# A smaller-products step at two places of a two-layer cross attention, with a bias sum moved to other engines and one load moved ahead

## The chip, the cores and the metric

The kernel runs on one core of one Trainium2 chip. The time is device time in microseconds (us) of one execution of the whole program, everything in float32. Five engines work side by side, each through its own queue in order: TensorE (PE, matrix products; its weight loads are shown apart as PEld), VectorE (DVE), ScalarE (ACT), GpSimd (POOL) and SyncE (SP, which here only issues DMA transfers). They wait for each other through semaphores. Sixteen DMA engines move data between the chip's memory (HBM) and the core's on-chip memory (SBUF).

## The reference

Eight batches of 100 tokens with 1024 features (x) attend twice to eight contexts of 1444 rows with 512 features (ctx). In short:

```python
Q, K, V = x @ Wq + bq, ctx @ Wk + bk, ctx @ Wv + bv        # layer 0, 1024 hidden
x = x + softmax(Q @ K.T / 32, over keys) @ V @ Wo + bo
q, k, v = x @ Wq1 + bq1, ctx @ Wk1 + bk1, ctx @ Wv1 + bv1  # layer 1
w = softmax(q @ k.T / 32, over the TOKENS)                 # axis=1
x = layernorm(w @ v + x) * gamma + beta
```

## The kernel before

The kernel never forms K or V. Scores are x Wq Wkᵀ ctxᵀ, so it multiplies the weights first (1024 x 512, one product per layer), applies that product to the tokens ("queries", called g here) and then multiplies g by the transposed context. The weighted rows of the context are multiplied afterwards by Wv Wo (another product of weights) in layer 0 and by Wv in layer 1. The biases give small additional vectors: of the key bias, the sum over h of WqT's rows times bk (1024 wide) is wanted in layer 0 only much later, as a bias of each token's scores.

The stages, in order of time:

- `qk0`, 0 to 53 us: the product of Wq and Wkᵀ of layer 0, while its weights load
- `vo0`, 53 to 99 us: the product of Wv and Wo of layer 0
- queries of layer 0, 99 to 135 us
- `qk1`, 135 to 182 us: the product of Wq and Wkᵀ of layer 1
- scores, softmax and weighted rows of layer 0 for the eight batches, 182 to 306 us. Scores of a later batch alternate with weighted rows of an earlier one
- projection by the product of Wv and Wo, 306 to 353 us, then queries of layer 1 up to 398 us, with the first batch's layer-1 scores in between
- the batches of layer 1, and a tail with the last layer norm up to 572 us

**Products by seven.** Each large product (weights or queries) is cut into 2 x 2 blocks A11 to A22 and B11 to B22 and done with seven block products instead of eight. The sums of blocks that this wants are called S1 to S4 (left) and T1 to T4 (right). The products have names that also show in the profile: X (first A11·B11, later more is accumulated on it), Z, Y = S1·T1, W, and the last one, called q. `put` copies a finished block from the accumulators to SBUF on ACT, `add` adds one on DVE. Some of the seven products are themselves done by seven smaller ones (`inner_product`), whose parts the profile shows as, for instance, `qk_q_x`, `qk_q_z` and so on. `half_steps` (L170) is the place that issues nearly all matmuls of products, so its line stands for all of them. `inner_product` yields after each smaller product, and `weight_products` uses that to interleave them with matmuls of another product (V). In `vo0` and `qk1` ("deep" in the code), Y is already done by seven smaller products. In `qk0` it is one product. In the queries of layer 1 the last product, S4·B22 added to Y (profile name g_y), is one product.

**Sums of scaled rows.** `scaled_copies` (L634) makes ACT write row times a scalar into one buffer each. `transfer_added` (L629) makes POOL issue a DMA from SBUF to SBUF that adds one buffer to another, 512 KB each time. `scaled_sum` builds a tree of these two. In `qk0` the first four of the key bias' eight terms go this way, and the other four are added on DVE (function `second_half`).

**What sets the order.** PE, ACT and POOL run in the order in which the program is written. DVE's order is chosen by a scheduler except where `vector.in_order` is set. SP issues loads in program order (`loaded_in_order`, L944), each waiting until its room in SBUF is free and until the transfers under way fit in 1800 KB. Rooms are taken from pools by tag: the eight weight rooms of `qk0` are followed by those of `vo0` (loads at L383 and L384, named vo in the profile), and those by the context's blocks (cT, transposed, four of them per batch, 128 features x 1444 rows each). `load_features(1, (2,))` loads the second batch's four blocks in the order 0, 1, 2, 3, where block 2 lies in a buffer of another tag (`prob`, three of them, also used by the bias sums).

Of the kernel before, what the change touches and what calls it, by code (L numbers as in the profile page):

```python
# [42 lines left out]
GT = G * T  # L43
TILES = ((0, 128), (128, 128), (256, 112), (368, 112), (480, 96), (576, 96), (672, 128))
SETS = ((2, (0, 1), range(0, 256)), (4, (2, 3), range(256, 480)), (6, (4, 5), range(480, 800)))
LATER = {(1, 4): 4, (1, 6): 4, (1, 7): 4}
ROWS = [range(8, 11), range(0, 4), range(4, 8)]
REST = range(11, 12)
FIRST, SECOND = (0, 3, 5), (1, 4, 6)
# [9 lines left out]
def two_layer_cross_attention(ctx: ExitStack, tc: tile.TileContext, a: dict, out: bass.AP):  # L59
# [294 lines left out]
    def weight_products(name, left, right, l_width, r_width, scaled, between=None):  # L354
# [32 lines left out]

        accs = {}

        def accumulate(side):  # L390
            for v, of in scaled:
                if of != side:
                    continue
                width = (l_width, r_width)[side]
                first = 0 if side == 0 else l_width
                srcs = [(units[h][:, first : first + width], cols[v][:, h : h + 1]) for h in range(EC)]
                if width == E:
                    accs[v] = transferred_sum(f"{name}_{v}", srcs, name)
                    continue
                acc = work.tile([P, L], F32, tag="half", name=f"{name}_{v}", bufs=1)  # L400
                accs[v] = acc
                if early:
                    tiles = [acc] + [t[:, i * L : (i + 1) * L] for t in prob for i in range(2)]
                    scaled_sum(tiles + [weight_rows(f"{name}_{v}_7")[:, :L]], srcs)
                    continue
                for h, (src, by) in enumerate(srcs):
                    if h == 0:
                        vector.tensor_scalar(acc, src, by, None, ALU.mult)
                    else:
                        vector.scalar_tensor_tensor(acc, src, by, acc, ALU.mult, ALU.add)  # L410
# [86 lines left out]
        if name == "qk0":  # L497

            t2, t4 = (weight_rows(f"{name}_t{n}") for n in (2, 4))
            T2, T4 = ([t[:, i * rh : (i + 1) * rh] for i in range(H)] for t in (t2, t4))  # L500
            Z = pair("z")
            product(Z, A12, B21, True)
            combine(T2, B22, T1, ALU.subtract)
            combine(T4, B21, T2, ALU.subtract)
            combine(S1, A21, A22, ALU.add)
            add(0, 0, Z)
            accumulate(1)
            W = pair("w")
            product(W, A22, T4, True)
            accumulate(0)  # L510
            put(1, 0, W)
        elif not deep:
            combine(S1, A21, A22, ALU.add)
            Z = pair("z")
            product(Z, A12, B21, True)
            accumulate(0)
        t = wide_sums(f"{name}_t")
        if deep:

            T2, S2, T4 = B11, A11, B21  # L520
            first, rest = slice(0, H - 1), slice(H - 1, H)
            combine(S1[first], A21[first], A22[first], ALU.add)
            for some in (first, rest):
                if some is rest:
                    combine(S1[some], A21[some], A22[some], ALU.add)
                combine(B12[some], B22[some], B12[some], ALU.subtract)
                combine(T2[some], B22[some], T1[some], ALU.subtract)
            Z = pair("z")
            product(Z, A12, B21, True)
            next(side, None)  # L530
            combine(A21, A11, A21, ALU.subtract)
            combine(S2, S1, A11, ALU.subtract)
            V = half_steps(X, S2, T2, False, nb, rh)
            for n, _ in enumerate(inner_product(f"{name}_y", S1, T1, nb, rh, t[:, 768:1536], *parts(1, 1))):
                run(islice(V, 2 * nb // (2 if n == 1 else 4)))
                if n == 1:
                    add(0, 0, Z)
                elif n == 3:
                    combine(T4, B21, T2, ALU.subtract)
                if n > 2:  # L540
                    next(side, None)
            run(V)
            put(0, 1, X)
        else:
            Y = pair("y")
            product(Y, S1, T1, True)
            put(1, 1, Y)
            vector.in_order = name != "qk0"
            combine(B12, B22, B12, ALU.subtract)
            if name != "qk0":  # L550
                T2, T4 = B11, B21
                combine(T2, B22, T1, ALU.subtract)
                add(0, 0, Z)
            combine(S1, S1, A11, ALU.subtract)
            S2 = S1
            combine(A21, A11, A21, ALU.subtract)
            if name != "qk0":
                combine(T4, B21, T2, ALU.subtract)
            product(X, S2, T2, False)
            put(0, 1, X)  # L560
        vector.in_order = True
        if name == "qk0":
            accs[scaled[0][0]][1]()
        V = half_steps(X, A21, B12, False, nb, rh)
        _, more = parts(0, 1)

        def last():
            combine(A12, A12, S2, ALU.subtract)
            if deep:
                for j in range(2):  # L570
                    to = block(0, 1, j)
                    vector.tensor_tensor(to, to, block(1, 1, j), ALU.add)
            else:
                add(0, 1, Y)
            return inner_product(f"{name}_q", A12, B22, nb, rh, t[:, 768:1536], more, more)

        if name == "qk0":
            run(islice(V, 2 * nb))
# [21 lines left out]
    def transferred_sum(name, srcs, of):  # L600

        n = EC if of == "qk1" else EC // 2
        tiles = [row(f"{name}_{n}") for n in range(2)] + [weight_rows(f"{name}_2")[:, :E]]
        tiles += [t[:, :E] for t in prob]
        if of != "qk0":
            tiles += [weight_rows(f"{name}_{n}")[:, :E] for n in range(6, 8)]
        if of == "qk1":  # L610
            tiles = [tiles[i] for i in (0, 3, 1, 4, 2, 5, 6, 7)]
        scaled_sum(tiles[:n], srcs[:n])

        def second_half():
            t = tiles[n]
            if of != "qk0":
                scaled_sum(tiles[n:], srcs[n:])
            else:
                for i, (src, by) in enumerate(srcs[n:]):
                    if i == 0:  # L620
                        vector.tensor_scalar(t, src, by, None, ALU.mult)
                    else:
                        vector.scalar_tensor_tensor(t, src, by, t, ALU.mult, ALU.add)
            transfer_added(tiles[0], t)

        return tiles[0], second_half

    def transfer_added(to, t):
        nc.gpsimd.dma_start(out=to, in_=t, accum_op=ALU.add)  # L629
# [83 lines left out]
    def key_bias_rows(kb, part, bqbk):  # L713

        n = B * T // QD
        ps = bank("kb")[:, :n]
        for h in both_sides():
            nc.tensor.matmul(ps[h * HP : (h + 1) * HP], same[:, h * HP : (h + 1) * HP], part, start=True, stop=True)
        vector.tensor_scalar(part, ps, SCALE, bqbk, ALU.mult, ALU.add)
        spread = part.unsqueeze(2).to_broadcast([P, n, QD])  # L720
        vector.transpose(kb.rearrange("p (n i) -> p n i", i=QD), spread)

    def queries(layer, w, u, between=None):

# [42 lines left out]

        t = None

        def inner(n, lhs, rhs, put, add, right=None, at=0, left=None):  # L770
            spare = bank if layer else bank2
            return inner_product(f"g{layer}_{n}", lhs, rhs, nb, GT, t[:, at:], put, add, right, left, spare=spare)

        def four(t):

# [2 lines left out]
        def steps():  # L778
# [85 lines left out]
                vector.in_order = False  # L864
            else:
                run(V)
                add(1, 0, X)
                add(1, 1, X)
                vector.in_order = False
                yield  # L870
                product(Y, S4, B22, False)
                add(0, 1, Y)
            yield

        return dst, steps()
# [76 lines left out]
    def load_features(b, blocks=(2, 3), parts=2):  # L952

        bounds = [LAST * i // parts for i in range(parts)] + [S]

        for k in range(LC):
            name = f"cT_{b}_{k}"
            t = feature_block(name) if k in blocks else unit(name)[:, :S]
            for part in (slice(i, j) for i, j in zip(bounds, bounds[1:])):
# [585 lines left out]
                next(A, None)  # L1545
            yield

    cT = [list(load_features(0)), list(load_features(1, (2,)))]
    c0, more = list(load_rows(0)), load_features(2)
    cT.append([next(more)])  # L1550
    scores0 = scores_by_keys(batches[0], 0, cT[0], softmax0)
    run(islice(scores0, 3 * MC + 6))
    key_bias_rows(kb0, part0, bqbk0)
    run(scores0)
    cT[2] += more
    block_sums("u1", acc_u, sums[:, :LC, :], late=True)
# [40 lines left out]
    run(more)  # L1597
    vector.in_order = False
    part = key_bias_parts(kb1)
# [9 lines left out]
    tiles = [{"t0": t0, "n": n} for t0, n in TILES]  # L1609
    turned = turned_blocks(tiles)  # L1610
    scores1 = scores_by_keys(batches[0], 1, cT[0], softmax1, hold=True)
    run(islice(scores1, LC * MC))
    key_bias_rows(kb1, part, bqbk1)
    run(scores1)
    run(steps)
    run(scores_by_keys(batches[1], 1, cT[1], softmax1))

    finished = {
# [67 lines left out]
```

## Time and profile before

| | |
|---|---|
| runs | 573.16, 574.49, 570.84 us (median 573.16) |
| profiled execution | 574.2 us, its span 572.4 us |
| granted TensorE clock | 0.996 |
| PE busy | 561.5 us (98%) |
| DVE, ACT, POOL busy | 447.5, 146.0, 113.0 us |
| DMA moved | 141.24 MB, mean 247 GB/s |

The span runs from the first to the last recorded instruction; the execution's own time is 1.8 us longer. Busy time of an engine is the time in which at least one of its instructions ran. A row like `25.75 6.91 PE qk_y L170 x32` in the chain of waits reads: from 25.75 us on, for 6.91 us, the chain lies on 32 matmul records of PE that write the tile qk_y, issued at line 170. Each float32 matmul stands as two records. A group such as `vo<-vo,vo 128x512 f32<-128x512 f32` reads: output tile, then inputs, then shapes as partitions x elements; in brackets stands idle time before it and what ended it. In rows by window the figures are the stretch and its sum, then busy time of PE, PEld, DVE, ACT and POOL in us with the number of instructions, then the clock, the mean busy share of the 16 DMA engines, and GB/s.

### The profile page before, as it was taken

Reading aid. Unit: us, or ns where it says so; the run is one execution under the profiler, and the core shown is the slowest. Engines: PE = TensorE matmul, PEld = TensorE weight load, DVE = VectorE, ACT = ScalarE, POOL = GpSimd, SP = SyncE. Lnnn points to the kernel's source line nnn. Section 1 sums busy time; section 2 is a strip of 40 time slices with the busy share of each in tenths; the row PEclk is TensorE's granted clock in tenths of the full one; section 3 lists DMA queues with packets and bytes.
Section 4 is the critical chain, followed back from the end, with each engine's and each line's share of the span. In section 5 each row is a group of like instructions: output and inputs, shape, how many; then the busy total and the mean of one; then the engine's idle time right before and its main releaser. Section 6 shows DMA issues by size and latency. Waiting matters only on the chain.

```text
span 572.4 us, 17304 instructions
## 1 busy us (share of the span) xinstructions
PE 561.5 (98%) x7316; PEld 470.1 (82%) x7316; DVE 447.5 (78%) x1035; ACT 146.0 (26%) x383; POOL 113.0 (20%) x171
## 2 busy tenths in 40 slices
PE   9999999999999999999999999999999999999994
PEld 8888567668999999999998856678999869959672
DVE  1996979878989794976458687796688779879865
ACT  1331321356020112222011000122333035336632
POOL 3110110223100043242122000000421312403232
PEclk9999999999999999999999999999999999999998
DMA  8959989958839999999999603985799969985804
GB/s 278 315 110 326 315 197 285 320 87 198 212 58 321 351 314 318 316 338 308 309 319 347 209 1 134 281 297 189 232 301 331 334 226 330 300 279 169 216 8 92
DMA packets 73390, 141.24 MB, mean 247 GB/s; under 512 B 8160, under 2 KB 29920, under 8 KB 73312
## 3 DMA queue, kind: packets, MB, share of 16 engines
q1 hardware_dynamic: 66592, 121.40, 63.1%
q0 software_dynamic: 6288, 18.20, 16.4%
q8 instruction: 58, 0.95, 0.7%
q10 hardware_dynamic: 432, 0.52, 0.3%
q14 instruction: 20, 0.16, 0.1%
HBM read 123.49 MB, written 6.03 MB: 226 GB/s over the span
## 4 chain that ended last, share of the span: by engine, by line
PE 84%; DMA 10%; issue 1%; DVE 1%; POOL 1%; ACT 1%; SPq 1%; DVEq 0%; POOLq 0%
PE s L1087 17%; PE A L1015 16%; DMA cT<-in_ctxT 10%; PE qk_x L170 7%; PE g_x L170 6%; PE vo_x L170 4%; PE o_x L170 3%; PE g_y L170 3%; PE o_x L1338 3%; PE qk_z L170 2%; PE o_y L1338 2%; PE o_y L170 1%; PE qk_w L170 1%; PE qk_y L170 1%; PE vo_z L170 1%
## 5 line engine op out<-in xcount | busy, mean ns | idle before, releaser
L1015 PE MATMUL A<-w,c 128*64 128x100 f32 (+2 forms) x3072 | 216.9, 249 | 0.0
L1015 PEld LDWEIGHTS A<-w,c 128*64 128x64 f32 (+2 forms) x3072 | 190.8, 137 | 3.0 <-issue 1.8
L1087 PE MATMUL s<-g0T,cT 128*64 128x100 f32 (+1 forms) x1472 | 108.9, 249 | 2.2 <-DMA cT<-in_ctxT 1.5
L1087 PE MATMUL s<-g1T,cT 128*64 128x100 f32 (+1 forms) x1472 | 109.4, 249 | 0.0
L1087 PEld LDWEIGHTS s<-g0T,cT 128*64 128x64 f32 (+1 forms) x1472 | 95.1, 136 | 2.9 <-DMA cT<-in_ctxT 1.9
L1087 PEld LDWEIGHTS s<-g1T,cT 128*64 128x64 f32 (+1 forms) x1472 | 94.8, 136 | 1.1 <-issue 1.1
L1305 POOL TENSOR_TENSOR part<-w 128x500 f32<-128x500 f32 x16 | 25.3, 1582 | 237.8 <-DVE rtotal L102 75.8
L1283 ACT ACTIVATE w<-w,negmax 128x100 f32<-128x100 f32 x96 | 34.9, 365 | 45.0 <-DVE negmax L102 44.8
L1151 ACT ACTIVATE w<-w 128x400 f32<-128x400 f32 (+2 forms) x32 | 12.7, 446 | 116.4 <-DVE w L102 105.6
L102 DVE STREAM_TRANSPOSE z<-xT 32x256 f32<-32x256 f32 x88 | 38.3, 436 | 1.4
L170 PE MATMUL qk_x<-qk 128*128 128x256 f32 x160 | 38.0, 382 | 0.0
L170 PEld LDWEIGHTS qk_x<-qk 128*128 128x128 f32 x160 | 29.1, 192 | 3.5 <-ACT qk L444 0.2
L1068 DVE RECIPROCAL rrow<-A 128x100 f32<-128x100 f32 x8 | 6.1, 768 | 22.3 <-PE A L1059 22.3
L170 PE MATMUL vo_x<-vo 128*128 128x512 f32 x48 | 23.3, 594 | 0.0
L102 DVE TENSOR_REDUCE most<-s 128x100 f32<-128x400 f32 (+1 forms) x24 | 12.5, 524 | 12.1 <-PE s L1087 11.6
L102 DVE SCALAR_TENSOR_TENSOR w<-s,kb 128x400 f32<-128x400 f32 (+2 forms) x32 | 14.1, 464 | 8.2 <-PE s L1087 7.8
L102 DVE TENSOR_TENSOR w<-w,rtotal 128x400 f32<-128x400 f32 (+2 forms) x32 | 18.1, 566 | 1.1
L1283 ACT ACTIVATION_READ_ACCUMULATOR w<-w,negmax 128x1 f32 x96 | 18.0, 187 | 0.0
L740 ACT ACTIVATE g1T<-g_x,k 128x400 f32<-128x400 f32 x4 | 2.4, 593 | 60.3 <-PE g_x L170 60.2
L1308 POOL TENSOR_TENSOR part<-part 128x100 f32<-128x100 f32 x32 | 15.8, 493 | 2.5
L102 DVE TENSOR_TENSOR qk<-qk 128x256 f32<-128x256 f32 (+2 forms) x26 | 14.4, 579 | 0.0
L170 PE MATMUL qk_z<-qk 128*128 128x256 f32 x64 | 14.1, 379 | 0.0
(484 smaller groups left out, 1001.7 us busy)
## 6 DMA issues: line engine op xcount, KB each, us to landing
c<-in_ctx SPq DMA_DIRECT2D x176, 256.0 KB, 5.1
cT<-in_ctxT SPq DMA_DIRECT2D x96, 176.0 KB, 4.6
cT<-in_ctxT SPq DMA_DIRECT2D x32, 370.0 KB, 5.2
cT<-in_ctxT SPq DMA_DIRECT2D x32, 352.0 KB, 4.8
cT<-in_ctxT SPq DMA_DIRECT2D x32, 194.0 KB, 4.8
vo<-in_L_xattn_Wo SPq DMA_DIRECT2D x8, 512.0 KB, 8.7
qk<-in_L_xattn_WqT SPq DMA_DIRECT2D x8, 512.0 KB, 5.1
qk<-in_L_xattn_WqT SPq DMA_DIRECT2D x15, 256.0 KB, 5.0
```

What stands on the lines that cost most here:

```text
L102: ins = getattr(nc.vector, op)(*args, **kw)
L170: nc.tensor.matmul(banks[n // per][:, n % per * width : (n % per + 1) * width], lhs[i][:, n * P : (n + 1) * P], rhs[i], start=(fresh and i ...
L740: nc.scalar.activation(dst[g][:, c, :], banks[j][:, :GT], AF.Identity, bias=u[:, c : c + 1])
L1015: nc.tensor.matmul(ps[h * HP : (h + 1) * HP, k * T : (k + 1) * T], block[rows, m % CQ, k * P + h * HP : k * P + (h + 1) * HP], s["w"][rows ...
L1068: nc.vector.reciprocal(r, ps[:, GT : GT + T])
L1087: nc.tensor.matmul(to, cT[k][:, o : o + n], q[:, k, t0 : t0 + T], start=(k == 0 and m % GM == 0), stop=(k == LC - 1 or (k == LC - 2 and no ...
L1151: nc.scalar.activation(rows, rows, AF.Exp)
L1283: ins = nc.scalar.activation(rows[:, i, :], rows[:, i, :], AF.Exp, bias=negmax[:, i : i + 1], accum_out=total[:, i : i + 1])
L1305: add(part, w[:, 0:5, :], w[:, 5:10, :], ALU.add)
L1308: add(part[:, 0, :], part[:, 0, :], more, ALU.add)
L1338: nc.tensor.matmul(ps[:n, :], lhs[0][:, i, :], rhs[0][:, i, :], start=(fresh and i == 0), stop=(i == 1), skip_group_check=True,)
```

## The change

There are four parts.

1. In `qk0` the product Y is done by seven smaller products, interleaved with the next one (X += S2·T2), in the way the deep stages do it. S2 and the small sums get rooms of their own (three more `wide_sums` buffers in turn). The last product's sum `add(0, 1, Y)`, from the accumulators, becomes a sum of two SBUF blocks. The second bias, bq, is summed in two halves of four terms.
2. The key bias' second four terms go from DVE to ACT (four scaled copies into `prob1`, `prob2`, `prob0` and a row buffer) and POOL (four accumulating transfers, where there was one), issued piece by piece between the smaller products. In all of this bias' sum there are seven such transfers instead of four.
3. The second batch's third key block (index 2) is loaded first; the order on SP is 2, 0, 1, 3.
4. In the queries of layer 1 the last product is done by seven smaller ones. The key bias' rows are made four scores earlier, and the first batch's softmax runs between the smaller products and not inside the scores.

```diff
-LATER = {(1, 4): 4, (1, 6): 4, (1, 7): 4}
+LATER = {(1, 0): 0, (1, 4): 4, (1, 6): 4, (1, 7): 4}
...
-            Y = pair("y")
-            product(Y, S1, T1, True)
-            put(1, 1, Y)
-            vector.in_order = name != "qk0"
-            combine(B12, B22, B12, ALU.subtract)
...
-            combine(S1, S1, A11, ALU.subtract)
-            S2 = S1
-            combine(A21, A11, A21, ALU.subtract)
...
-            product(X, S2, T2, False)
+            vector.in_order = True
+            late = accs[scaled[0][0]][1]()
+            rooms = [wide_sums(f"{name}_s2_{i}") for i in range(2)]
+            S2 = [t2[:, i * lh : (i + 1) * lh] for t2 in rooms for i in range(2)]
+            combine(S2, S1, A11, ALU.subtract)
+            Y = inner_product(f"{name}_y", S1, T1, nb, rh, t[:, 768:1536], *parts(1, 1))
+            V = half_steps(X, S2, T2, False, nb, rh)
+            for n, _ in enumerate(Y):
+                run(islice(V, 2 * nb // (2 if n == 1 else 4)))
+                if n in (1, 2, 5):
+                    next(late)
+                if n == 3:
+                    combine(B12, B22, B12, ALU.subtract)
+                elif n == 4:
+                    accumulate(1, range(H, EC))
+                    combine(A21, A11, A21, ALU.subtract)
+            run(V)
             put(0, 1, X)
...
-        if name == "qk0":
-            accs[scaled[0][0]][1]()
...
+        def second_half_in_turn():
+            t, u, v, w = tiles[n], tiles[n + 1], tiles[n - 1], tiles[1]
+            scaled_copies((t, u), srcs[n : n + 2])
+            transfer_added(t, u)
+            yield
+            scaled_copies((v,), srcs[n + 2 : n + 3])
+            yield
+            scaled_copies((w,), srcs[n + 3 :])
+            for to, src in ((v, w), (t, v), (tiles[0], t)):
+                transfer_added(to, src)
+            yield
...
-                product(Y, S4, B22, False)
-                add(0, 1, Y)
+                _, more = parts(0, 1)
+                Q = inner("q", S4, B22, more, more, four(T2[0]), ahead=True)
+                yield
+                yield from Q
...
-    cT = [list(load_features(0)), list(load_features(1, (2,)))]
+    cT = [list(load_features(0))]
+    block, *more = load_features(1, (2,), order=(2, 0, 1, 3))
+    cT.append([*more[:2], block, *more[2:]])
...
-    run(islice(scores1, LC * MC))
-    key_bias_rows(kb1, part, bqbk1)
+    rows = key_bias_rows(kb1, part, bqbk1)
+    run(islice(scores1, LC * (MC - 1)))
+    next(rows)
+    run(islice(scores1, LC))
+    vector.in_order = True
+    next(steps)
+    run(rows)
+    next(steps)
     run(scores1)
+    first_softmax = batches[0]["softmax"]
+    for n in (1, 2, 2, 1):
+        next(steps)
+        run(islice(first_softmax, n))
+    next(steps)
+    vector.in_order = False
     run(steps)
+    run(first_softmax)
```

More of the change, by code (lines that the diff above doesn't have):

```diff
@@ L388, in weight_products, with accumulate @@
         accs = {}
-        def accumulate(side):
+        def accumulate(side, some=range(EC)):
             for v, of in scaled:
@@ L399, in accumulate @@
                     continue
-                acc = work.tile([P, L], F32, tag="half", name=f"{name}_{v}", bufs=1)
-                accs[v] = acc
+                if some[0] == 0:
+                    accs[v] = work.tile([P, L], F32, tag="half", name=f"{name}_{v}", bufs=1)
+                acc = accs[v]
                 if early:
@@ L405, in accumulate @@
                     continue
-                for h, (src, by) in enumerate(srcs):
+                for h in some:
+                    src, by = srcs[h]
                     if h == 0:
@@ L506, in weight_products @@
             add(0, 0, Z)
-            accumulate(1)
+            accumulate(1, range(H))
             W = pair("w")
@@ L511, in weight_products @@
             put(1, 0, W)
[L512 to L516, printed above, removed]
         t = wide_sums(f"{name}_t")
@@ L544, in weight_products @@
         else:
-            Y = pair("y")
-            product(Y, S1, T1, True)
-            put(1, 1, Y)
-            vector.in_order = name != "qk0"
-            combine(B12, B22, B12, ALU.subtract)
[L550 to L553, printed above, removed]
-            combine(S1, S1, A11, ALU.subtract)
-            S2 = S1
-            combine(A21, A11, A21, ALU.subtract)
-            if name != "qk0":
-                combine(T4, B21, T2, ALU.subtract)
-            product(X, S2, T2, False)
+            vector.in_order = True
[15 more added lines that the diff above has]
+            run(V)
             put(0, 1, X)
         vector.in_order = True
-        if name == "qk0":
-            accs[scaled[0][0]][1]()
         V = half_steps(X, A21, B12, False, nb, rh)
@@ L568, in last @@
             combine(A12, A12, S2, ALU.subtract)
[L569 to L573, printed above, removed]
-                add(0, 1, Y)
-            return inner_product(f"{name}_q", A12, B22, nb, rh, t[:, 768:1536], more, more)
+            for j in range(2):
+                to = block(0, 1, j)
+                vector.tensor_tensor(to, to, block(1, 1, j), ALU.add)
+            room = t if deep else wide_sums(f"{name}_q_t")
+            return inner_product(f"{name}_q", A12, B22, nb, rh, room[:, 768:1536], more, more)
         if name == "qk0":
@@ L614, in second_half @@
         def second_half():
[L615 to L626, printed above, removed]
+            scaled_sum(tiles[n:], srcs[n:])
+            transfer_added(tiles[0], tiles[n])
+        def second_half_in_turn():
[9 more added lines that the diff above has]
+            yield
+        return tiles[0], second_half_in_turn if of == "qk0" else second_half
     def transfer_added(to, t):
@@ L721, in key_bias_rows @@
         vector.transpose(kb.rearrange("p (n i) -> p n i", i=QD), spread)
+        yield
     def queries(layer, w, u, between=None):
@@ L768, in queries, with inner @@
         t = None
-        def inner(n, lhs, rhs, put, add, right=None, at=0, left=None):
-            spare = bank if layer else bank2
-            return inner_product(f"g{layer}_{n}", lhs, rhs, nb, GT, t[:, at:], put, add, right, left, spare=spare)
+        def inner(n, lhs, rhs, put, add, right=None, at=0, left=None, ahead=False):
+            spare = bank if layer and not ahead else bank2
+            return inner_product(f"g{layer}_{n}", lhs, rhs, nb, GT, t[:, at:], put, add, right, left, ahead, spare)
         def four(t):
@@ L866, in steps @@
                 run(V)
+                add(0, 1, Y)
                 add(1, 0, X)
@@ L870, in steps @@
                 yield
-                product(Y, S4, B22, False)
-                add(0, 1, Y)
+                _, more = parts(0, 1)
+                Q = inner("q", S4, B22, more, more, four(T2[0]), ahead=True)
+                yield
+                yield from Q
             yield
@@ L950, in loaded_in_order, with load_features @@
             tc.add_manual_dep(load, latest.name, landed, reason="room among the transfers under way")
-    def load_features(b, blocks=(2, 3), parts=2):
+    def load_features(b, blocks=(2, 3), parts=2, order=range(LC)):
         bounds = [LAST * i // parts for i in range(parts)] + [S]
-        for k in range(LC):
+        for k in order:
             name = f"cT_{b}_{k}"
@@ L1552, in two_layer_cross_attention @@
     run(islice(scores0, 3 * MC + 6))
-    key_bias_rows(kb0, part0, bqbk0)
+    run(key_bias_rows(kb0, part0, bqbk0))
     run(scores0)
@@ L1597, in two_layer_cross_attention @@
     run(more)
+    part = key_bias_parts(kb1)
+    next(steps)
     vector.in_order = False
-    part = key_bias_parts(kb1)
     wv1 = weights.tile([P, LC, E], F32, tag="w", name="wv1")
@@ L1611, in two_layer_cross_attention @@
     scores1 = scores_by_keys(batches[0], 1, cT[0], softmax1, hold=True)
-    run(islice(scores1, LC * MC))
-    key_bias_rows(kb1, part, bqbk1)
-    run(scores1)
+    rows = key_bias_rows(kb1, part, bqbk1)
[6 more added lines that the diff above has]
+    next(steps)
+    run(scores1)
+    first_softmax = batches[0]["softmax"]
+    for n in (1, 2, 2, 1):
+        next(steps)
+        run(islice(first_softmax, n))
+    next(steps)
+    vector.in_order = False
     run(steps)
+    run(first_softmax)
     run(scores_by_keys(batches[1], 1, cT[1], softmax1))
```

## The prediction

> **What bounds the kernel now.** I read the busy rows first, then TensorE's waits, then the chain that ended last, then the stages that the change touches, by window. Busy rows of the page:
>
> ```profile
> PE 561.5 (98%) x7316; PEld 470.1 (82%) x7316; DVE 447.5 (78%) x1035; ACT 146.0 (26%) x383; POOL 113.0 (20%) x171
> ```
>
> TensorE (PE) works 98% of the 572.4 us span. Its waits are all of this (engine, line, what it waited for: us in total, times, longest):
>
> ```profile
> PE s L1087 <- DMA cT<-in_ctxT: 1.5, 2, 0.9
> PE warm L114 <- DVE ones L111: 1.1, 1, 1.1
> PE s L1087 <- issue: 0.6, 1, 0.6
> PE ol L1498 <- ACT A1T L1030: 0.4, 1, 0.4
> ```
>
> 3.6 us in all. So the time falls only where matmuls go, and rises where a new wait appears. The stretches of the chain that the change replaces (start, us, what):
>
> ```profile
> 25.75 6.91 PE qk_y L170 x32
> ...
> 48.33 0.89 PE qk_q_y L170 x8
> ...
> 129.92 0.68 PE g_q_x L170 x4
> ...
> 392.50 5.57 PE g_y L170 x16
> ```
>
> Rows 1 and 4 are the two products that become seven smaller ones; rows 2 and 3 are one such smaller product of each width.
>
> **First stage, the product itself.** 32 records of 128x256 (6.91) become seven groups like row 2: 7 x 0.89 = 6.25 us. -0.66. Here a rule speaks against the change: the Trainium skill, "TensorE: Matmul & The Clock Gate", section "Back-to-back issue gap", gives about 81 ns per matmul at 128 columns and 131 at 512, so narrow ones cost nearly as much as wide ones. Interpolated (an estimate: 98 ns at 256), 56 narrow records against 32 would be 56 x 81 / (32 x 98) = 1.45 times, 6.91 to 10.0, +3.1. In the rows a record falls from 0.216 to 0.112 with half the columns, and the same exchange is seen in the second layer's first product. I take the rows.
>
> The seven are interleaved with the next product, so their sums must keep up. The key bias leaves VectorE (DVE): one of 0.66 and three of 1.20, 4.26 us between 31.3 and 36.9. What comes is some 14 sums, half of them 128x256 at 0.34 and half 128x128 at 0.20, 3.8 us, and two block sums of 0.34 for two sums of 0.60 gone. Replayed in order with these durations, the tightest sum is 2.8 us ahead of its matmul. ScalarE (ACT) takes four of 1.05; its copy of a smaller product stands behind the one that waits for a transfer landing at 33.3, and ends at about 34.7, 2.4 us ahead of need. No stall: 7 groups and the rest end 0.66 earlier, at about 52.1.
>
> **Its three further transfers.** The bias is now summed by accumulating DMAs of 512 KB that GpSimd (POOL) issues: seven, four before. This stage loads the next weights (vo) meanwhile. DMA shares, windows with start:end, then PE, PEld, DVE, ACT, POOL busy, clock, DMA share, GB/s:
>
> ```profile
> 36.00:42.00 6.00, 6.00 (x29) 5.06 (x28) 5.82 (x12) 2.99 (x4) 0.86 (x1) 1.00 0.63 119
> 42.00:48.00 6.00, 6.00 (x37) 5.46 (x36) 2.54 (x9) 1.42 (x2) 0.86 (x1) 1.00 1.01 248
> 48.00:54.00 6.00, 6.00 (x48) 5.43 (x48) 5.16 (x13) 1.15 (x1) 0.86 (x1) 1.00 1.00 381
> 54.00:62.00 8.00, 8.00 (x20) 3.54 (x19) 8.00 (x18) 2.66 (x4) 0.00 (x0) 1.00 1.01 289
> 62.00:66.00 4.00, 4.00 (x11) 1.78 (x10) 3.82 (x10) 2.68 (x3) 2.42 (x3) 1.00 1.05 397
> ```
>
> Up to 42 there is room, then the engines are full to past 66. From 34 to 42.4 two transfers took 66.0% of 8.4 us, 2.8 us of all engines each. The order of POOL's queue after: two old ones by 33.3, prob1+=prob2 at about 34, prob0+=bk1 at 36 (these fill the room), prob1+=prob0 once both landed, about 43, then bv0+=bv1 (42.56 before, now behind that wait), bk0+=prob1 after the landing before it, about 50, then bv2+=prob0 (53.03 before). So two extra, 5.5 us of DMA time, fall into full engines, beside vo_4 to vo_7, the last issued at 52.81. That one is waited for at once:
>
> ```profile
> 62.46 0.69 DVE L102 TENSOR_TENSOR vo<-vo,vo 128x512 f32<-128x512 f32 x1 [0.18 <-DMA vo<-in_L_xattn_Wo]
> ```
>
> It lands at 62.4. DVE needs 2.9 us more for the sum S2, so PE could have it at 65.4; PE wants it at 67.46 (66.8 with the 0.66 gained). PE then waits D = L - 63.9, L the landing. The skill's "DMA: Bandwidth & Descriptors", section "Issuing engines are not separate DMA queues", says that DMAs of all issuers interleave on the same 16 engines; the trace agrees (shares of both queues sum to 1.0), so the extra transfers do take from the loads. How much: from 42.4 to 62.4 the loads used 72.9% and the transfers 27.7%, 14.6 and 5.5 us. If both extra ones go ahead wholly, L = 67.9, D = 4.0; if bv2+=prob0 is pushed behind vo_7 in turn (2.6 us of it were served before 62.4), L = 65.3, D = 1.4; if the transfers starve while loads are queued, as from 50 to 57 where only loads moved, L stays near 62 and D = 0. I take the middle of the upper two, D = 2.3: prob1+=prob0 surely goes ahead (the window 46 to 48 had 88% for transfers while loads were queued), bk0+=prob1 in part. Bounds 0 and 4.0. Below nothing is excluded: the loads gain nothing.
>
> **Second batch's third key block first.** SyncE (SP) now sits 26.9 us at the block it loads first, while this stretch passes:
>
> ```profile
> 165.00:170.00 5.00, 5.00 (x36) 4.69 (x35) 5.00 (x15) 0.74 (x2) 0.00 (x0) 1.00 0.00 0
> ```
>
> No DMA at all. The block loaded first has a room free at about 142.2, so its 739 KB (2.1 us at the 345 GB/s of this stage's full slices) move out of the later stream. But PE waits for no DMA until 285.2; its two waits there (1.5 us) follow back through transfers to a room that PE itself frees at 230.4. Between is a stretch that is 0.96 full (190 to 300). Bounds: 0, and -1.5 if the stream runs ahead. I take 0, since the chain starts at a room and not at a transfer before it. The block competes with the second layer's key-bias load (issued 143.3, read at 156.1 by DVE): up to 2 us later, into 1.8 us of DVE idle at 158.2. Nothing.
>
> **Second layer, last product.** 5.57 becomes 7 x 0.68 = 4.76: -0.81. Sums added on DVE: four of 0.34 and four of 0.49, 3.3 us, after the key bias' row sums that end at 388.9 and with the softmax of the first batch moved behind, between the products. Replayed, the last three operands are ready 0.4 to 0.9 us ahead of PE. That margin is thin: the same form in this layer's z group took 5.14 where it waited for DVE, so the bound is -0.4. The key-bias matmul wants its input 1.7 us after it is ready; the softmax ends at about 403.5, before the weighted rows want it at 405.2. I take -0.81.
>
> **Sum.** -0.66 + 2.3 + 0 - 0.81 = +0.8. The profiled execution took 574.2 (572.4 and 1.8 around it), so 575.0; on the median of the three runs, 573.16, it is 574.0. A difference within 1% is what a measurement of this kernel can't tell from none.
>
> **Rivals.**
>
> A. As summed, some of the two transfers ahead of vo_7: D 1.0 to 4.0, 572.7 to 575.7. Chance 0.5.
>
> B. The transfers are hidden: D near 0. 573.16 - 1.47 = 571.7, and to 570.2 if the early block also takes away the waits at 285 and 294. For it: transfers got nothing from 50 to 57, and both landed late rather than the loads (10.0 us for bv2+=prob0). Against it: 46 to 48. Chance 0.32.
>
> C. Slower: ACT's in-order queue. Its copy prob1<-vo (60.41) must now wait until bk0+=prob1 has been read from prob1. Behind it stand four bias copies of 1.09 and then the copy of vo_y_x, at 67.66. If that transfer lands at time K, the copy comes at K + 4.4, and the products that read it move. It decides from K = 63.3, and beyond it each us costs PE one. Issued at 50 and taking 10 as bv2+=prob0 did, K = 60; served last, after 11 us of transfers and 14.6 of loads from 42.4, K = 68, and where packets of both go slower than apart (the shares run to 1.05), 71: D = 7.7, net +6.2, 579.4. Chance 0.15.
>
> D. The seven products do not pay: in the first stage a group waits for ACT's copy behind the transfer (slack 2.4), in layer two for DVE. Both gains gone with D = 2.3: 575.5. Chance 0.03, and inside the range.
>
> **Range.** 570.5 to 577.8: B's no-wait end at the bottom, and at the top A with D = 4 and 2 us more for the partly decided C. Left out are C's upper end and the best of B. Slower by over 1% (above 578.9) needs C fully: 0.10. Faster by over 1% (below 567.4) needs more than all gains together: 0.02.
>
> **What would show it.** The y groups with the interleaved product should stand from 25.75 to about 38.9 without a wait; no g_y row of 5.57 but seven of 0.68 near 392. DVE's wait for vo_7 should move from 62.46 to 64.9 to 67.9, followed by a new PE wait at vo_x of 1 to 4 us. If that wait is missing, B holds. If PE waits at the vo_y products for ACT, C holds. DMA should show a block of 739 KB soon after 143 and the wait of 26.9 us on SP should stay, at another block. Wrong would be: waits inside the seven products, DMA waits in the first layer's batches that grow because rooms come free in another order, or a clock below 0.996.

## The result, and the profile after

The changed kernel takes 577.63 us (median of 7 runs, 574.78 to 578.11) against 573.16 us before (7 runs, 570.84 to 575.31). The ratio is 1.0068, with a 95% interval of 1.0048 to 1.0089. By this ratio, which all the runs go into, it is slower by about 3.9 us (2.8 to 5.1); the two medians alone are 4.5 us apart. That is inside the range that was forecast and on the side of the forecast, but far more than the +0.8 us of its sum. The profiled execution has a span of 574.7 us, 2.3 us longer than before. That execution took 576.56 us, 1.1 us less than the median of its kernel; the profiled one of before took 1.0 us more than the median of its own.

First the busy row of the page, then TensorE's waits in the changed kernel (engine, line, what it waited for: us in total, times, longest):

```profile
PE 561.1 (98%) x7352; PEld 472.0 (82%) x7352; DVE 454.3 (79%) x1067; ACT 151.0 (26%) x389; POOL 115.8 (20%) x174
```

```profile
PE vo_z L170 <- DMA vo<-in_L_xattn_Wo: 1.9, 1, 1.9
PE vo_x L170 <- DVE vo L102: 1.3, 1, 1.3
PE warm L114 <- DVE ones L111: 1.1, 1, 1.1
PE g_x L170 <- ACT prob L633: 0.6, 1, 0.6
PE s L1091 <- DMA cT<-in_ctxT: 0.5, 1, 0.5
```

The first two rows are new: 3.2 us in the product of Wv and Wo, at two places. The waits for DMA in the first layer's batches are down from 1.5 to 0.5 us. The chain of waits shows the new stretch (start, us, what):

```profile
26.14 0.89 PE qk_y_x L170 x8
27.03 0.87 PE qk_x L170 x4
27.90 0.89 PE qk_y_z L170 x8
...
51.64 13.21 DMA vo<-in_L_xattn_Wo
64.85 0.14 issue
64.98 1.97 PE vo_z L170 x4
66.95 0.03 issue
66.98 0.69 DVE vo L102
67.67 0.34 DVE vo_s L102
68.01 2.89 DVE vo L102 x7
70.90 0.14 issue
71.03 1.10 PE vo_x L170 x2
```

The smaller products run without a wait. Then a load of Wo, issued at 51.64, needs 13.2 us to land, and after it the sums on DVE are late too. DVE itself, in order of time (start, us, engine, line, operation, tiles; in brackets the idle time before and what ended it):

```profile
56.98 0.76 DVE L102 TENSOR_TENSOR vo_s<-vo,vo 128x256 f32<-128x256 f32 x2
63.63 0.42 DVE L102 TENSOR_TENSOR vo_s<-vo,vo 128x256 f32<-128x256 f32 x1 [5.89 <-DMA vo<-in_L_xattn_WvT]
63.98 1.89 DVE L102 TENSOR_TENSOR vo<-vo,vo 128x512 f32<-128x512 f32 x3
65.78 1.89 DVE L102 TENSOR_TENSOR vo<-vo,vo_s 128x512 f32<-128x512 f32 x3
67.59 0.42 DVE L102 TENSOR_TENSOR vo_s<-vo,vo 128x256 f32<-128x256 f32 x1
67.92 0.68 DVE L102 TENSOR_TENSOR vo<-vo,vo 128x512 f32<-128x512 f32 x1
```

The third sum of this kind, which wants the WvT half of vo_6 (issued at 51.26), makes DVE stand still for 5.89 us. Before, the three sums ran without a wait:

```profile
57.25 1.09 DVE L102 TENSOR_TENSOR vo_s<-vo,vo 128x256 f32<-128x256 f32 x3
```

Everything behind the wait in DVE's order is late, down to the operand S2 that PE wants. By window (stretch, sum, busy us of PE, PEld, DVE, ACT, POOL with counts, clock, DMA share, GB/s), the same stretches as in the prediction:

```profile
36.00:42.00 6.00, 6.00 (x36) 5.32 (x35) 5.15 (x11) 2.60 (x4) 0.86 (x1) 1.00 1.04 196
42.00:48.00 6.00, 6.00 (x37) 5.49 (x36) 4.39 (x15) 2.30 (x2) 1.71 (x2) 1.00 0.94 280
48.00:54.00 6.00, 6.00 (x47) 5.28 (x46) 5.42 (x14) 1.15 (x1) 1.71 (x2) 1.00 1.05 256
54.00:62.00 8.00, 8.00 (x20) 3.41 (x19) 3.74 (x9) 2.69 (x4) 0.00 (x0) 1.00 1.06 298
62.00:66.00 4.00, 2.10 (x6) 0.76 (x5) 2.37 (x5) 1.74 (x2) 1.45 (x2) 1.00 1.03 368
```

The DMA engines were as full before from 42 on; what changed is whom they serve. In the list of queues, cut to 42.4 to 62.4 us (queue: packets, MB, share of 16 engines), before and then after:

```profile
q1 hardware_dynamic: 1962, 5.09, 72.9%
q0 software_dynamic: 297, 1.05, 27.7%
```

```profile
q1 hardware_dynamic: 1349, 3.65, 52.3%
q0 software_dynamic: 541, 2.01, 50.4%
```

The first queue holds the loads, the second POOL's transfers. The transfers' part rises from 5.5 to 10.1 us of all engines, and 1.44 MB of loads no longer arrive in this time.

Where the profile's 2.3 us went, by the start of the first matmul at each mark, after minus before: -0.3 at the start of the vo stage, +3.7 at the first vo_w_x, +4.4 at the second g_x product, +4.7 at the first weighted row, +2.4 at the projection of layer 0, +1.8 at the first weighted row of layer 1, +2.3 at the end. So from Z on the first stage gains 0.7 (Z itself came 0.4 later), the vo stage loses 3.9, the queries and the second product of weights 1.0, the batches of layer 0 give 2.3 back, and the last product of layer 1's queries 0.6.

### The profile page after: what moved, and what is told of

Read it like the earlier page. It is cut to its first block, busy times and chain, and to the rows that moved or that the text cites. A ratio compares the mean times of both kernels' runs of the same rounds, so it can differ in the third digit from the quotient of the medians.

```text
span 574.7 us, 17432 instructions
## 1 busy us (share of the span) xinstructions
PE 561.1 (98%) x7352; PEld 472.0 (82%) x7352; DVE 454.3 (79%) x1067; ACT 151.0 (26%) x389; POOL 115.8 (20%) x174
## 4 chain that ended last, share of the span: by engine, by line
PE 83%; DMA 10%; DVE 2%; issue 1%; ACT 1%; POOL 1%; SPq 0%; DVEq 0%; POOLq 0%; ACTq 0%
PE s L1091 19%; PE A L1019 18%; PE qk_x L170 7%; DMA cT<-in_ctxT 7%; PE g_x L170 5%; PE o_x L170 3%; PE o_x L1342 3%; PE vo_x L170 2%; PE qk_z L170 2%; DMA vo<-in_L_xattn_Wo 2%; PE o_y L1342 2%; PE g_y L170 2%; PE o_y L170 1%; PE qk_w L170 1%; DMA qk<-in_L_xattn_WkT 1%
## 5 line engine op out<-in xcount | busy, mean ns | idle before, releaser
L102 DVE TENSOR_TENSOR qk<-qk 128x256 f32<-128x256 f32 (+2 forms) x29 | 16.0, 585 | 0.0
L628 POOL DMA_DIRECT2D qk_L_xattn_bk<-qk_L_xattn_bk x6 | 5.2, 923 | 44.5 <-ACT qk_L_xattn_bk L633 17.6
```

The source lines that it names most:

```text
L102: ins = getattr(nc.vector, op)(*args, **kw)
```

## The experiments

My theory after the result: the further transfers push vo's loads back, and all of the loss is in that. Rivals: the seven smaller products and the sums moved around them cost it; and the regained 2.3 us in layer 0's batches come from the load order, or only from PE being late. For the part that is in question, one number is read from the profile of every run: the stretch from the first vo_x to the first vo_w_x, by the tile's rows. It is 26.7 us before and 30.6 in the changed kernel, and what is gained or lost earlier or later does not enter it directly. The ratios are to the kernel before.

**The bias part alone.** To the kernel before, only this:

```diff
             put(1, 1, Y)
+            if name == "qk0":
+                run(accs[scaled[0][0]][1]())
...
+        def second_half_in_turn():
+            t, u, v, w = tiles[n], tiles[n + 1], tiles[n - 1], tiles[1]
+            scaled_copies((t, u), srcs[n : n + 2])
+            transfer_added(t, u)
...
```

> The kernel before with the second part alone: the key bias' last four terms by ACT and seven accumulating transfers, Y still one product. Transfers theory (the three further 512 KB transfers push back the loads of vo): PE waits at vo_z and vo_x for about 3 to 4 us in all, the whole is 3.5 to 5 us slower (ratio 1.006 to 1.009). Rival (the loss comes from the seven smaller products and the new order of sums around them): within 0.7 us of before, no wait at vo_z.

Measured: 1.0103 (1.0069 to 1.0137), 5.9 us slower, more than the 3.5 to 5 that were expected, and the stretch is 32.0 us, 5.3 more. TensorE's waits:

```profile
PE vo_z L170 <- DMA vo<-in_L_xattn_Wo: 3.0, 2, 2.3
```

The rival falls: with one large Y the loss is there. The changed kernel's 3.9 us are less than these 5.9 by about what its other parts give (0.7 and 0.6 us in the profiles of the two products, and something for the order). In this kernel ACT's four copies are issued after the whole of Y, so the first two late transfers start at 36.66 and 38.73 (33.29 and 36.67 in the changed kernel); whether that makes the stretch longer was not tried, and it is within 0.5 us of the changed kernel's in its second profile below.

**Two transfers less.** The changed kernel, with the loop over the last sums cut:

```diff
-            for to, src in ((v, w), (t, v), (tiles[0], t)):
+            for to, src in ((v, w),):
```

> The changed kernel, leaving out two accumulating transfers of the key bias in the first stage (prob1+=prob0 and bk0+=prob1), so that half of that bias' terms are missing from its sum. Transfers theory: the loads of vo land as before the change, PE's waits at vo_z and vo_x are gone, 3 to 4.5 us faster than the changed kernel (ratio to before 0.996 to 1.000). Rival (seven smaller products): still 3 us or more slower than before.

Measured: 0.9976 (0.9960 to 0.9992). The stretch is 27.4 us, and no wait at vo_z is left. Faster than before by 1.4 us, faster than the changed kernel by 5.3 us (1.0068 - 0.9976 of 573). So these two transfers, with what waits for them, turn a gain into a loss; nothing else of the change was taken out here.

**One transfer less.**

```diff
-            for to, src in ((v, w), (t, v), (tiles[0], t)):
+            for to, src in ((v, w), (t, v)):
```

> The changed kernel leaving out one accumulating transfer (bk0+=prob1), so the key bias lacks half of its terms. Two transfers less gave 5.3 us against the changed kernel. If each pushes the loads by its 2.7 us of DMA time (transfers theory): between, 2 to 3.3 us faster than the changed kernel, ratio to before 0.999 to 1.003, a wait of about 1 us at vo_z or vo_x. If only the last one matters: as fast as with both left out (0.9976). If only the first: as slow as the changed kernel (1.007).

Measured: 1.0008 (0.9991 to 1.0025); the stretch is 28.8 us. TensorE's waits there:

```profile
PE vo_x L170 <- DVE vo L102: 0.9, 1, 0.9
PE vo_z L170 <- DMA vo<-in_L_xattn_Wo: 0.5, 2, 0.3
```

With none, one and two of these transfers the whole is at -1.4, +0.5 and +3.9 us, and the stretch at 27.4, 28.8 and 30.6. So each costs. The second step looks larger than the first, but the intervals of the totals don't separate them.

**POOL adds in place of transfers.** The changed kernel with three of the four late sums as instructions on POOL:

```diff
-            transfer_added(t, u)
+            tc.keep_in_program_order(nc.gpsimd.tensor_tensor(t, t, u, ALU.add))
...
-            for to, src in ((v, w), (t, v), (tiles[0], t)):
-                transfer_added(to, src)
+            for to, src in ((v, w), (t, v)):
+                tc.keep_in_program_order(nc.gpsimd.tensor_tensor(to, to, src, ALU.add))
+            transfer_added(tiles[0], t)
```

> The changed kernel with three of its four late accumulating transfers of the key bias done as additions on POOL (128x1024 each, by the 1.58 us of a 128x500 addition of POOL some 3.2 us each); the last, into bk0, stays a transfer, so there are four in all as before the change. Transfers theory: the vo loads land about as before the change, no wait at vo_z, 3 to 5 us faster than the changed kernel and 0.5 to 1.5 us faster than before (ratio 0.997 to 0.999). Rival (POOL's additions slow DVE or hold bv0+=bv1 up): DVE rows of the first stage longer than in the changed kernel, or vo waits of 1 us or more remain; ratio 1.001 or more.

Measured: 1.0068 (1.0039 to 1.0098), as slow as the changed kernel, for another reason. The stretch is 26.7 us: the vo loads are on time for PE. But the first stage, from the start of Z to the first vo_x, is 5.2 us longer than in the changed kernel, and the rows of POOL, DVE and PE say why:

```profile
33.48 2.68 POOL L616 TENSOR_TENSOR prob<-prob,prob 128x1024 f32<-128x1024 f32 x1
36.18 2.75 POOL L622 TENSOR_TENSOR prob<-prob,qk_L_xattn_bk 128x1024 f32<-128x1024 f32 x1
39.01 2.67 POOL L622 TENSOR_TENSOR prob<-prob,prob 128x1024 f32<-128x1024 f32 x1
```

```profile
32.20 7.28 DVE L102 SCALAR_TENSOR_TENSOR qk_L_xattn_bq<-qk,L_xattn_bq,qk_L_xattn_bq 128x512 f32<-128x512 f32 x4
39.41 4.64 DVE L102 TENSOR_TENSOR qk<-qk 128x512 f32<-128x512 f32 x4
```

```profile
42.38 5.38 PE L170 MATMUL qk_x<-qk 128*128 128x256 f32 x16 [3.36 <-DVE qk L102]
```

The same two groups of four DVE operations took 3.11 and 2.49 us in the changed kernel. DVE loses 6.3 us beside 8.1 us of additions by POOL. PE waits 3.4 us for it, and its next 16 records take 5.38 us where they took 3.69 in the changed kernel. A single DVE operation lasts up to 2.83 us, about as long as one addition of POOL. The rival that I had put down for this run holds. The Trainium skill, "SBUF — State Buffer", section "Who interferes with whom", has the rule: a DVE instruction with two inputs in SBUF contends with a GpSimd instruction that reads SBUF, since the two engines share a port pair that is an exclusive lock. The trace agrees: all eight of these DVE operations read two inputs from SBUF, and their time grew from 5.60 to 11.92 us.

**The bias left on DVE.** The changed kernel with its second part undone:

```diff
-            scaled_copies((t, u), srcs[n : n + 2])
-            transfer_added(t, u)
-            yield
...
+            for i, (src, by) in enumerate(srcs[n:]):
+                if i == 0:
+                    vector.tensor_scalar(t, src, by, None, ALU.mult)
+                else:
+                    vector.scalar_tensor_tensor(t, src, by, t, ALU.mult, ALU.add)
...
```

> The changed kernel with its second part undone: the last four terms of the key bias on DVE (one of 0.66 and three of 1.20 us, between the smaller products), four transfers. Transfers theory: no wait at vo_z; DVE's 4.3 us less the 2.8 us that its sums were ahead leave a PE wait of up to 1.5 us among the smaller products of the first stage, total 573 (ratio 0.997 to 1.001). Rival (moved sums elsewhere are the loss): 1.005 or more.

Measured: 1.0020 (1.0004 to 1.0036), just beyond what was expected at the upper end. The stretch is 26.7 us, without a vo_z wait. PE waits for DVE in the first stage instead (waits up to 60 us):

```profile
PE qk_q_x L170 <- DVE qk L102: 0.8, 1, 0.8
PE qk_x L170 <- DVE qk L102: 0.4, 1, 0.4
```

That is 1.2 us, within the 1.5 that the slack of DVE left. But the stage from Z to the first vo_x takes 42.4 us, where it took 41.0 before and 40.4 in the changed kernel: with the bias on DVE the seven smaller products cost 1.3 us instead of gaining 0.7. So they do need the bias to leave DVE there, or most of it. Behind vo, the queries and the second product of weights take 1.6 us longer than before, although no further transfers run in this kernel.

**The last two sums on DVE, later.** The changed kernel with the two late transfers as two DVE additions, placed where DVE idles:

```diff
-            for to, src in ((v, w), (t, v), (tiles[0], t)):
-                transfer_added(to, src)
-            yield
+            transfer_added(v, w)
+            yield
+            vector.tensor_tensor(t, t, v, ALU.add)
+            vector.tensor_tensor(tiles[0], tiles[0], t, ALU.add)
+            yield
...
         next(Q)
+        if name == "qk0":
+            next(late)
         run(V)
```

> The changed kernel with its last two sums of the key bias (prob1+=prob0, bk0+=prob1) as two DVE additions of 128x1024 (1.2 us each) at about 45 to 47.5 us, where DVE idles, and the other two late ones still as transfers before 43 us. Nothing is left out. Transfers theory: as with both transfers left out, no wait at vo_z, ratio to before 0.996 to 0.999. Rival (any work in this place delays the last product's sums): a PE wait of 1 us or more at qk_q, ratio 0.999 to 1.002.

Measured: 0.9973 (0.9959 to 0.9988), 572.30 us. All terms of the sum are there. The stretch is 26.7 us. The two additions on DVE, and below them the queues from 42.4 to 62.4 us; PE has no wait in this stage:

```profile
46.79 1.22 DVE L102 TENSOR_TENSOR prob<-prob,prob 128x1024 f32<-128x1024 f32 x1
48.04 1.23 DVE L102 TENSOR_TENSOR qk_L_xattn_bk<-qk_L_xattn_bk,prob 128x1024 f32<-128x1024 f32 x1
```

```profile
q1 hardware_dynamic: 1892, 4.98, 71.5%
q0 software_dynamic: 289, 1.05, 27.4%
```

The queues' shares are those of the kernel before within 1.5 points. This version beats both kernels.

**The load order.** Three runs bear on it: the third part alone on the kernel before,

```diff
...
-    cT = [list(load_features(0)), list(load_features(1, (2,)))]
+    cT = [list(load_features(0))]
+    block, *more = load_features(1, (2,), order=(2, 0, 1, 3))
+    cT.append([*more[:2], block, *more[2:]])
```

> The kernel before with the third part alone: block 2 of the second batch loaded first. Order theory: PE's waits for DMA at 285 and 294 us shrink or go, 1 to 2 us faster (ratio 0.996 to 0.998). Rival (those waits went in the changed kernel because PE came there some 4 us later, and the loads didn't): they stay, within 0.5 us of before.

the changed kernel with the old order,

```diff
-    block, *more = load_features(1, (2,), order=(2, 0, 1, 3))
-    cT.append([*more[:2], block, *more[2:]])
+    cT.append(list(load_features(1, (2,), order=(0, 1, 2, 3))))
```

> The changed kernel with the second batch's blocks loaded in the old order. Order theory: 1 to 2 us slower than the changed kernel (ratio to before 1.008 to 1.010), DMA waits of 1 us or more between 240 and 310 us. Rival (the order makes no difference): 1.006 to 1.008.

and the same edit on the version with the last two sums on DVE:

> The run before, with the second batch's blocks loaded in the old order. If the order is worth something where PE is not late: 1 us or more slower than that run. If it is worth nothing: within 0.5 us of it.

Measured: 0.9992 (0.9974 to 1.0010) for the order alone; 1.0088 (1.0060 to 1.0115) against 1.0064 for the changed kernel, measured again below; 0.9979 (0.9961 to 0.9997) against 0.9973. All three differences favour the new order, by 0.5, 1.4 and 0.3 us, and each lies within its interval. Parts three and four together against part four alone (both below) make a fourth, 1.0 us the same way and within its interval too. From the first weighted row to the projection of layer 0 the nine profiles with the new order take 103.4 to 107.2 us (mean 104.9), the five with the old one 105.4 to 106.8 (mean 106.0). One of the new order, with one transfer less, has a 2.1 us wait for DMA there. So a gain of about 1 us or less is likely and not shown. Of the 2.3 us that the changed kernel's profile regained in these batches about 1 may be the order; the rest is scatter between profiles.

**The last product of layer 1's queries alone.** The kernel before with the fourth part, as the diff of the change has it.

```diff
...
-                product(Y, S4, B22, False)
-                add(0, 1, Y)
+                _, more = parts(0, 1)
+                Q = inner("q", S4, B22, more, more, four(T2[0]), ahead=True)
...
```

> The kernel before with the fourth part alone: the last product of layer 1's queries by seven smaller ones. By the sum of the prediction: 0.8 us faster, seven groups of 0.68 at about 392 us. Rival (the early key-bias matmul and the moved softmax give it back): the groups without a wait, but at the end no difference, or slower.

Measured: 0.9989 (0.9970 to 1.0007). The total can't tell it from none, but the profile can: from the first g_w_x to the first weighted row of layer 1 it takes 31.25 us, as in the changed kernel, where it took 31.85 before. The gain is 0.6 us. The chain of the changed kernel there:

```profile
394.24 0.72 PE s L1091 x16
394.96 0.87 PE g_q_x L170 x4
395.83 0.68 PE g_q_z L170 x4
...
399.21 0.68 PE g_q_x L170 x4
```

The first of the seven has 0.87 for 0.68, so they take 4.93 us, from 394.96 to 399.89, and not the 4.76 of the sum.

**Parts three and four together**, both diffs on the kernel before:

> The kernel before with the load order and the last product of layer 1 only. The two alone measured 0.9992 and 0.9989; if they add: 0.998 of before, and 0.7 us slower than with the first stage's seven products without late transfers.

Measured: 0.9971 (0.9956 to 0.9986), 571.71 us. It also beats both kernels, and was not 0.7 us behind the version with the seven products of the first stage: their medians are 0.6 us apart the other way, and the intervals overlap almost wholly. The first stage's gain is plain in the profile (from the start of Z to the first vo_x: 41.0 us before, 40.4 in the changed kernel, 40.5 with the last two sums on DVE), but that much can't be seen in the total. No version with the seven products of the first stage was measured faster than this one without them.

**The changed kernel again**, beside these runs:

> The changed kernel itself, on the chip of the three runs above: 1.005 to 1.009 of before, its PE waits at vo_z and vo_x 3 us or more in all.

Measured: 1.0064 (1.0040 to 1.0088), the stretch 31.5 us. Its waits in the vo stage are one row, a little less than the 3 us that were expected:

```profile
PE vo_z L170 <- DMA vo<-in_L_xattn_Wo: 2.8, 1, 2.8
```

## Why the prediction came out as it did

- First stage, -0.66: right, in number and in kind. The stretch from Z to the first vo_x fell from 41.0 to 40.4 us (by 0.65), with no wait among the smaller products. A record of 128 columns took 0.111 us and one of 256 columns 0.217, so half the columns cost half, and the +3.1 that I had estimated from the rule on narrow matmuls did not come.
- Removing DVE's part of the key bias: right that the sums keep up. The run with the bias on DVE shows what that saved: its first stage is 2.0 us longer than the changed kernel's, 1.2 us of it as recorded waits.
- The transfers, D = 2.3: the mechanism was right, the size was not. D is 3.9 in the changed kernel's first profile, 4.8 and 4.2 in two others (one with the old order), at the upper bound of 4.0 or beyond it. There was a slip in the sum: the middle of 4.0 and 1.4 is 2.7 and not 2.3, which makes the total +1.2 and not +0.8. Two steps failed besides. "bk0+=prob1 in part": the transfers took 10.1 us of DMA time where 5.5 were before, so 4.5 of the extra 5.5 us went ahead. And "DVE needs 2.9 us more" after vo_7 lands: that was counted from the last load, while DVE takes its sums in order and stood at the WvT half of vo_6 until 63.6, with 7.3 us of sums up to S2 behind it. DVE never waited for vo_7 in this profile. PE's first wait was one that I had no term for, at vo_z for the Wo half of vo_6, 1.9 us.
- Load order, 0: the sum took none and bounds of 0 to -1.5; the runs favour a small gain. The block came later than I had read off: it was issued at 151.3 us and not soon after 143, and SP then waited 22.4 us at the next block, where it had waited 26.9.
- Layer 1's product, -0.81: right in kind, 0.6 in size, as the first group takes 0.87 us and not 0.68.
- Some 0.9 to 1.6 us after the vo stage was not foreseen. From the first g_x to the first weighted row the changed kernel took 1.0 us longer than before, 0.9 in its second profile and 1.6 in the run with the old order; of this the queries up to the second g_x have 0.7, 0.3 and 1.6, and in the run with the old order PE waits 0.9 us there for the transfer that fills g_t. The runs do not tie this to the further transfers of the bias: the kernel with the bias part alone has all of them and loses nothing there (100.8 us, 101.0 before), and the one with the bias left on DVE has none and loses 1.6. Its cause stays open.
- The range held in part by luck. Rival A, which is the mechanism that came true, ended at 575.7; 573.16 times the ratio is 577.1, and the median is 577.63. Both are covered only by the 2 us that were added for rival C, and C did not happen.
- A clock below 0.996 was named as a sign of being wrong. The changed kernel's profile has 0.995, but its runs lie between 0.994 and 0.998, and runs of the kernel before between 0.993 and 0.998, so this sign says nothing here.

Of the rivals, B (the transfers are hidden) falls: no transfer starves. The gap from 50 to 57 that spoke for it was the time from a transfer's issue, 53.03, to its first packets. In the changed kernel the transfer issued at 52.04 has no packet from 55 to 56 and 71.5% of the engines in the next us. C (ACT's queue) falls: bk0+=prob1 landed at 60.4, below the 63.3 from which it decides, and ACT's copy behind it started 0.07 us later than before:

```profile
60.48 2.19 ACT L633 ACTIVATE prob<-vo,L_xattn_bv 128x1024 f32<-128x1024 f32 x2 [0.23 <-DMA qk_L_xattn_bk<-prob]
```

That this meets the K = 60 that was worked out is luck: the transfer was issued at 52.0 and not at 50, and took 8.4 us and not 10. D falls too: no wait is recorded in either set of seven products.

The sum with the measured terms: -0.7 in the first stage, +3.9 to +4.8 in vo, +0.9 to +1.6 behind it, -0.3 to -1.4 for the order (not shown to differ from none), -0.6 in layer 1, together +2.1 to +4.8; the measured total is +3.9, with an interval of +2.8 to +5.1.

## What to carry to other kernels

A transfer between buffers on the chip is work for the same DMA engines as the loads, so before moving a sum from an engine to DMA, look at the share of the DMA queues in the stretch where it will run, and give it a price where that is 1.0. Ask also whether the engine that it leaves needs the room: the seven smaller products gained only with the bias off DVE. When a load comes later, find the first consumer of every part of it and what is queued in order behind that consumer; the last load to land is not always the one that sets the time. A few additions on an engine with a gap at that moment (here DVE, 2.4 us) were cheaper than the transfers, and than additions on POOL that slowed a busy DVE.

## What the hardware showed that I had not expected

- Where both queues have packets, transfers and loads move nearly the same number of packets and hold very different shares of the time. From 56 to 62 us of the changed kernel:

```profile
q0 software_dynamic: 235, 0.90, 74.7%
q1 hardware_dynamic: 260, 0.68, 31.6%
```

By packet an accumulating transfer held an engine 2.6 times as long as a load there, and by byte 1.8 times. Two other such stretches agree in the packets: 107 and 118 from 50.4 to 53 in the changed kernel, 107 and 108 from 45.2 to 48 before. So once a transfer has its first packets, the loads beside it are left with about a quarter to a third of the engines.
- With the engines full of loads, a transfer's first packets came 2.2 to 4.8 us after its issue (before: issued at 42.56 and 53.03, first packets from 44.8 and 57.8; changed kernel: 43.47 and 52.04, from 47.0 and 56.0), and then it took most of the engines. With no load under way it was 1.3 us (before: issued at 38.34, from 39.6).
- Three additions of 128x1024 on POOL (2.7 us each) went with 6.3 us more of DVE's time for the same eight operations.
- The first part of the first product, from the first qk_x to the first qk_z, scatters from 6.9 to 8.2 us over the profiles, though no run changes it, so that stages are better compared from a mark behind it.
